# A selected-weight residual product on one core: the weights in eight transfers, the last stores in pairs

## The chip, the core and the metric

The kernel runs on one NeuronCore of a Trainium2 chip. The core has a TensorE (PE) for matrix products, a VectorE (DVE), a ScalarE (ACT), a GpSimd (POOL) and a SyncE (SP), each with its own instruction stream. Data moves between HBM and the on-chip memory SBUF (128 partitions) by 16 DMA engines, which all queues share. Here SyncE issues the small loads and all stores, ScalarE issues all loads of `x`. The metric is the device time of one execution in microseconds.

## What is computed

```python
def reference(x, itok_B_0_7, L0_cond_weights):
    # x (128, 128, 1024) f32, itok_B_0_7 (128,) int32 in 0..7, weights (8, 128, 128) f32
    w = L0_cond_weights[itok_B_0_7]
    return x + jnp.einsum('bct,bcd->bdt', x, w)
```

For each of 128 batch entries a 128 x 1024 matrix `x[b]` is multiplied by one of eight 128 x 128 weight matrices, chosen by the entry's index, and the product is added to `x[b]`. The input and the output are 67.1 MB each.

## The kernel before

A tile is H x G = 2 x 2 matrices of `x`, 2 MB, 16 KB in each of the 128 partitions. There are NT = 32 tiles and SLOTS = 12 slots in SBUF (`x_all`), which the tiles take in turn. The sum is written in place: a slot is loaded, the products are added into it, and it is stored from there.

All waits between engines are written out by hand with semaphores:

- **Loads** (L200 to L204, on ScalarE's queue). Each matrix is a transfer of 512 KB of its own, `load`, taken from HBM in 32 runs of 16 KB. From tile 12 on, the loads of tile i wait until the slot's last store, that of tile i - 12, has landed. So the stores of tiles 0 to 19 are waited for by loads, those of tiles 20 to 31 are not.
- **Ready** (L206 to L211, GpSimd): waits for a tile's loads and tells TensorE.
- **Weights** (L181): all eight matrices, 512 KB, are loaded once at the start into `w_all`, by one transfer on SyncE, in rows of 512 B. VectorE waits for it at L222, then copies the chosen matrices into `ws` (`place`, L153).
- **Products** (`multiply`, L162): for each half tile (two matrices) four products into PSUM. **Adds** (`add`, L174): VectorE adds a half tile of 128 x 2048 from PSUM into the slot and counts it in `s_added`; then it places the next weights.
- **Stores** (L213 to L218, on SyncE's queue). Tile i's store (2 MB) waits in `s_added` for tile i + BEHIND, four tiles further, as long as i is under NT - BEHIND - 2 = 26. Tiles 26 to 30 wait for themselves alone, but are behind tile 25's store in the queue. The last tile is stored in three parts: 1 MB (two matrices) after its first half's add, 0.5 MB after its second, and the last matrix, 0.5 MB, by L238.
- **End** (L235 to L245): ScalarE waits for each of the last twelve slots' stores, and the program's end waits for the last one.

Engines issue in their own program order, so what is behind a wait on SyncE waits too. `transfer` (L52) is the helper through which loads and stores are issued; their recorded line is L59, that of the helper.

Of the kernel before, what the change touches and what calls it, by code (L numbers as in the profile page):

```python
# [30 lines left out]
G = 2  # L31
H = 2
# [5 lines left out]
P_SLOTS = 2  # L38

BEHIND = 4  # L40

DMA = 16

IDLE = 3

ROWS = 4

ALIGN = 4096
QUEUES = {mybir.EngineType.SP: "qSPDynamicHW", mybir.EngineType.Activation: "qActDynamicHW"}
# [2 lines left out]
def transfer(nc, engine, out, in_):  # L52

    later, nc._always_lower_symbolic_ap = nc._always_lower_symbolic_ap, False
    ins, outs = engine.lower_ap_dma(in_), engine.lower_ap_dma(out)
    nc._always_lower_symbolic_ap = later
    return engine.add_instruction(  # L59
        mybir.InstDMACopy(  # L60
            name=nc.get_next_instruction_name(),
            engine=engine.engine,
            ins=ins,
            outs=outs,
            mode="Copy",
            cce_op=ALU.bypass,
            queue=QUEUES[engine.engine],
        )
    )


@with_exitstack
def kernel(
    ctx: ExitStack,
    tc: tile.TileContext,
    x: bass.AP,
    subjects: bass.AP,
    weights: bass.AP,
    out: bass.AP,
):  # L80
    nc = tc.nc
    B, C, T = x.shape
    S, _, D = weights.shape
    NT = B // (G * H)

    def sbuf(name, *shape, dtype=F32):
        return ctx.enter_context(nc.sbuf_tensor(name, list(shape), dtype)).ap()


    room = -(nc.sbuf_base + -nc.sbuf_base % 32) % ALIGN  # L90
    if room:
        sbuf("room", C, room // 4)
    x_all = sbuf("x_all", C, SLOTS * H * G * T)
    xs = [
        x_all[:, i * H * G * T : (i + 1) * H * G * T].rearrange("c (q t) -> c q t", t=T)
        for i in range(SLOTS)
    ]
    w_all = sbuf("w_all", C, S, D)
    ws = [sbuf(f"w{i}", C, 1, D) for i in range(H * G)]
    zeros = sbuf("zeros", C, N)  # L100
    given, near, wrap = (sbuf(name, 1, B, dtype=I32) for name in ("given", "near", "wrap"))
    index = sbuf("index", 1, B + H * G, dtype=I32)
    ps = [
        ctx.enter_context(nc.psum_tensor(f"ps{i}", [D, G, T], F32)).ap() for i in range(P_SLOTS)
    ]

    s_given = tc.alloc_semaphore("s_given")
    s_wall = tc.alloc_semaphore("s_wall")
    s_index = tc.alloc_semaphore("s_index")
    s_zeros = tc.alloc_semaphore("s_zeros")  # L110
    s_product = tc.alloc_semaphore("s_product")
    s_added = tc.alloc_semaphore("s_added")

    s_ready = tc.alloc_semaphore("s_ready")
    s_go = tc.alloc_semaphore("s_go")

    s_slot = [tc.alloc_semaphore(f"s_slot{k}") for k in range(SLOTS)]
    s_head = tc.alloc_semaphore("s_head")

    def emptied(i):  # L120
        turns = i // SLOTS
        return DMA * (H * G + 1) * turns - (DMA * G if i >= SLOTS and i % SLOTS == 0 else 0)

    def load(engine, i, q):
        transfer(
            nc,
            engine,
            xs[i % SLOTS][:, q, :],
            x[i * H * G + q].rearrange("(a r) t -> a (r t)", r=ROWS),
        ).then_inc(s_head if i * H * G + q < G else s_slot[i % SLOTS], DMA)  # L130

    def store(i, q0, q1):
        b = i * H * G
        transfer(
            nc,
            nc.sync,
            out[b + q0 : b + q1].rearrange("g d t -> d g t"),
            xs[i % SLOTS][:, q0:q1, :].rearrange("d (o g) t -> d o (g t)", g=q1 - q0),
        ).then_inc(s_slot[i % SLOTS], DMA)

    def subjects_of(i):
        _, subject = nc.values_load_multi_w_load_instructions(
            index[0:1, i] if isinstance(i, slice) else index[0:1, bass.ds(i * (H * G), H * G)],
            engines=[mybir.EngineType.DVE],
            min_val=0,
            max_val=S - 1,
            skip_runtime_bounds_check_because="the index is clamped on the chip above",
        )
        return subject

    def place(h, subject):
        for q in range(h * G, (h + 1) * G):
            copy = nc.vector.tensor_copy(ws[q], w_all[:, bass.ds(subject[q], 1), :])  # L153
        copy.then_inc(s_go, 1)

    def multiply(slot, h):
        nc.tensor.wait_ge(s_go, 1).then_inc(s_go, -1)
        nc.tensor.wait_ge(s_ready, 1).then_inc(s_ready, -1)  # L158
        for q in range(h * G, (h + 1) * G):
            for t in range(0, T, N):  # L160
                at = slot * (H * G * T) + (q * T + t)
                mm = nc.tensor.matmul(  # L162
                    ps[h][:, q % G, t : t + N],
                    ws[q][:, 0, :],
                    x_all[:, bass.ds(at, N)],
                    start=True,
                    stop=True,
                )
        mm.then_inc(s_product, 1)

    def add(slot, h):
        mine = x_all[:, bass.ds(slot * (H * G * T) + h * G * T, G * T)]
        nc.vector.wait_ge(s_product, 1).then_inc(s_product, -1)  # L173
        nc.vector.tensor_tensor(  # L174
            mine, ps[h].rearrange("d g t -> d (g t)"), mine, ALU.add
        ).then_inc(s_added, 1)

    with tc.tile_critical():  # L178

        nc.sync.dma_start(given, subjects.rearrange("(o b) -> o b", o=1)).then_inc(s_given, DMA)  # L180
        nc.sync.dma_start(w_all, weights.rearrange("s c d -> c s d")).then_inc(s_wall, DMA)  # L181

        nc.vector.memset(zeros, 0.0).then_inc(s_zeros, 1)  # L183
        nc.tensor.wait_ge(s_zeros, 1)
        for _ in range(IDLE):
            nc.tensor.matmul(  # L186
                ps[P_SLOTS - 1][:, G - 1, :N], zeros[:, :D], zeros, start=True, stop=True
            )

        nc.vector.memset(index[:, B:], 0).then_inc(s_index, 1)  # L193
        nc.vector.wait_ge(s_given, DMA)
        nc.vector.tensor_scalar(near, given, -S, S - 1, ALU.max, ALU.min).then_inc(s_index, 1)  # L195
        nc.vector.wait_ge(s_index, 2)
        nc.vector.tensor_scalar(wrap, near, 0, S, ALU.is_lt, ALU.mult).then_inc(s_index, 1)  # L197
        nc.vector.wait_ge(s_index, 3)
        nc.vector.tensor_tensor(index[:, :B], near, wrap, ALU.add).then_inc(s_index, 1)  # L199
        for i in range(NT):  # L200
            if i >= SLOTS:
                nc.scalar.wait_ge(s_slot[i % SLOTS], emptied(i))
            for q in range(H * G):
                load(nc.scalar, i, q)  # L204

        for i in range(NT):  # L206
            if i == 0:
                nc.gpsimd.wait_ge(s_head, DMA * G).then_inc(s_ready, 1)
                nc.gpsimd.wait_ge(s_slot[0], DMA * G).then_inc(s_ready, 1)
            else:  # L210
                nc.gpsimd.wait_ge(s_slot[i % SLOTS], emptied(i) + DMA * H * G).then_inc(s_ready, H)  # L211

        for i in range(NT):  # L213
            behind = BEHIND if i < NT - BEHIND - 2 else 0
            for h in range(H):
                if i == NT - 1 or h == H - 1:
                    nc.sync.wait_ge(s_added, (i + behind) * H + h + 1)
                    store(i, h * G if i == NT - 1 else 0, (h + 1) * G - (i * H + h == NT * H - 1))  # L218


        nc.vector.wait_ge(s_index, 4)
        nc.vector.wait_ge(s_wall, DMA)  # L222
        subject = subjects_of(slice(0, H * G))
        for h in range(H):
            place(h, subject)
        with nc.vector.Fori(0, NT) as turn:  # L226
            subject = subjects_of(turn + 1)
            for h in range(H):
                add(turn % SLOTS, h)
                place(h, subject)  # L230
        with nc.tensor.Fori(0, NT) as turn:
            for h in range(H):
                multiply(turn % SLOTS, h)

    with tc.tile_critical() as waits:  # L235
        for i in range(NT - SLOTS, NT):
            nc.scalar.wait_ge(s_slot[i % SLOTS], emptied(i + SLOTS) + (DMA if i == NT - 1 else 0))
    last = nc.sync.dma_start(out[B - 1], xs[(NT - 1) % SLOTS][:, H * G - 1, :])  # L238

    tc.add_manual_dep(  # L240
        last.ins,
        waits.name,
        mybir.DependencyInfo(mybir.DependencyClass.NoSync, mybir.DependencyReason.SCHED_ONLY),
        reason="the end of the program waits for it",
    )  # L245
# [27 lines left out]
```

## Time and profile before

| what | value |
|---|---|
| time, median of 3 runs (lowest to highest) | 323.61 us (323.46 to 323.78) |
| the profiled execution: time | 323.36 us |
| the profiled execution: span from first to last instruction | 321.6 us |
| mean granted TensorE clock | 0.909 |
| PE busy | 250.4 us (78%) |
| DVE busy | 165.7 us (52%) |
| moved by DMA | 134.76 MB in 12083 packets, mean 419 GB/s |
| loads of `x` on ScalarE's queue | 128 of 512 KB, median 35.5 us from issue to landing |
| stores on SyncE's queue | 31 of 2 MB, 1 of 1 MB, 2 of 0.5 MB; those of 2 MB median 16.2 us to landing |
| load of the weights | 1 of 512 KB, 5.2 us to landing |

Busy times are shares of one span and overlap each other. A share of 16 engines is the time that a queue's packets took, summed over all DMA engines, as a share of 16 times the stretch. "To landing" runs from the issue of a transfer to the arrival of its last completion, the time spent behind other transfers included. DMA issues are not counted as busy time of the engine that issues them.

### The profile page before, as it was taken

Reading aid. Unit: us, or ns where it says so; the run is one execution under the profiler, and the core shown is the slowest. Engines: PE = TensorE matmul, PEld = TensorE weight load, DVE = VectorE, ACT = ScalarE, POOL = GpSimd, SP = SyncE. Lnnn points to the kernel's source line nnn. Section 1 sums busy time; section 2 is a strip of 40 time slices with the busy share of each in tenths; the row PEclk is TensorE's granted clock in tenths of the full one; section 3 lists DMA queues with packets and bytes.
Section 4 is the critical chain, followed back from the end, with each engine's and each line's share of the span. In section 5 each row is a group of like instructions: output and inputs, shape, how many; then the busy total and the mean of one; then the engine's idle time right before and its main releaser. Section 6 shows DMA issues by size and latency. Waiting matters only on the chain. (4 is left out here: it accounts for less than half of the span.)

```text
span 321.6 us, 2379 instructions
## 1 busy us (share of the span) xinstructions
PE 250.4 (78%) x518; PEld 102.7 (32%) x518; DVE 165.7 (52%) x202; POOL 0.2 (0%) x4
## 2 busy tenths in 40 slices
PE   6999999999979676864989748899957969649100
PEld 2444444444433232321434313344312424214000
DVE  2377667767773266156267544167735237562300
POOL 0000000000000000000000000000000000000000
PEclk9999999999998699799799998599989799997755
DMA  7999999999999999999999999999999999999997
GB/s 279 430 424 424 426 424 406 428 428 430 424 424 426 423 428 426 426 428 426 428 428 428 424 426 426 426 426 426 428 428 426 430 428 426 424 426 426 428 426 300
DMA packets 12083, 134.76 MB, mean 419 GB/s; under 512 B 2609, under 2 KB 3634, under 8 KB 3890
## 3 DMA queue, kind: packets, MB, share of 16 engines
q1 hardware_dynamic: 5938, 67.64, 49.7%
q10 hardware_dynamic: 6144, 67.12, 49.6%
q14 instruction: 1, 0.01, 0.0%
HBM read 67.63 MB, written 67.11 MB: 419 GB/s over the span
## 5 line engine op out<-in xcount | busy, mean ns | idle before, releaser
L162 PE MATMUL ps<-x_all,w 128*128 x512 | 244.9, 636 | 46.4 <-PEq L158 30.8
L174 DVE TENSOR_TENSOR x_all<-ps,x_all 128x2048 f32 x64 | 146.7, 2291 | 129.5 <-DVEq L173 129.5
L162 PEld LDWEIGHTS ps<-x_all,w 128*128 128x128 f32 x512 | 100.9, 202 | 191.2 <-issue 190.7
L153 DVE COPY w<-w_all 128x128 f32 x132 | 23.2, 218 | 4.4 <-DMA w_all<-in_L_cond_weights_dram 4.4
L186 PE MATMUL ps<-zeros 128*128 128x512 f32 x6 | 5.5, 1088 | 1.7 <-DVE zeros L183 1.7
L186 PEld LDWEIGHTS ps<-zeros 128*128 128x128 f32 x6 | 1.9, 330 | 3.7 <-issue 2.1
L183 DVE MEMSET zeros<- 128x512 f32 x1 | 0.5, 485 | 1.0 <-SPq L178 1.0
L195 DVE TENSOR_SCALAR near<-given 1x128 int32<-1x128 int32 x1 | 0.2, 214 | 0.6 <-DMA given<-in_itok_B_dram 0.6
L199 DVE CUSTOM_DVE_ANT_0 index<-near,wrap 1x256 uint16<-1x256 uint16 x1 | 0.3, 280 | 0.0
L197 DVE TENSOR_SCALAR wrap<-near 1x128 int32<-1x128 int32 x1 | 0.2, 216 | 0.0
L260 POOL MEMSET const-bfloat16-1.0<- 128x1 bf16 x1 | 0.1, 102 | 0.0
L260 POOL MEMSET const-uint8-127<- 128x1 uint8 x1 | 0.1, 102 | 0.0
L260 POOL MEMSET const-float32-0.0<- 128x1 f32 x1 | 0.1, 99 | 0.2 <-issue 0.2
L260 POOL MEMSET const-float32-1.0<- 128x1 f32 x1 | 0.1, 99 | 0.0
L260 DVE BASE_LOAD x1 | 0.0, 15 | 0.1
L193 DVE MEMSET index<- 1x4 int32 x1 | 0.1, 62 | 0.0
## 6 DMA issues: line engine op xcount, KB each, us to landing
x_all<-in_x_dram ACTq DMA_DIRECT2D x128, 512.0 KB, 35.5
out_dram<-x_all SPq DMA_DIRECT2D x31, 2048.0 KB, 16.2
out_dram<-x_all SPq DMA_DIRECT2D x1, 1024.0 KB, 20.5
out_dram<-x_all SPq DMA_DIRECT2D x2, 512.0 KB, 18.3
w_all<-in_L_cond_weights_dram SPq DMA_DIRECT2D x1, 512.0 KB, 5.2
given<-in_itok_B_dram SPq DMA_DIRECT2D x1, 0.5 KB
```

The source lines that it names most:

```text
L153: copy = nc.vector.tensor_copy(ws[q], w_all[:, bass.ds(subject[q], 1), :])
L162: mm = nc.tensor.matmul(ps[h][:, q % G, t : t + N], ws[q][:, 0, :], x_all[:, bass.ds(at, N)], start=True, stop=True,)
L174: nc.vector.tensor_tensor(mine, ps[h].rearrange("d g t -> d (g t)"), mine, ALU.add).then_inc(s_added, 1)
L183: nc.vector.memset(zeros, 0.0).then_inc(s_zeros, 1)
L186: nc.tensor.matmul(ps[P_SLOTS - 1][:, G - 1, :N], zeros[:, :D], zeros, start=True, stop=True)
L193: nc.vector.memset(index[:, B:], 0).then_inc(s_index, 1)
L195: nc.vector.tensor_scalar(near, given, -S, S - 1, ALU.max, ALU.min).then_inc(s_index, 1)
L197: nc.vector.tensor_scalar(wrap, near, 0, S, ALU.is_lt, ALU.mult).then_inc(s_index, 1)
L199: nc.vector.tensor_tensor(index[:, :B], near, wrap, ALU.add).then_inc(s_index, 1)
L260: nc = _bacc.Bacc("TRN2", target_bir_lowering=False, num_devices=1)
```

## The change

The weights are loaded by eight transfers of 64 KB, one for each matrix, on the same queue. Each is read from HBM in 16 runs of 4 KB (eight rows of 512 B each) and written to one row of 512 B in each of 128 partitions. VectorE waits for all eight.

`store` now covers n whole tiles. Tiles 0 to 19 are stored one by one and wait as before for four tiles further. Tiles 20 to 31 are stored in pairs of neighbouring slots, 4 MB each. Pairs 20 and 22 wait for the fourth tile behind the pair's own last one (tiles 25 and 27); pairs 24, 26, 28 and 30 wait for their own adds alone. The last pair, tiles 30 and 31, is the program's last transfer, so the split of the last tile into three parts goes. ScalarE's waits at the end are five, one for each pair before the last.

```diff
@@ -38,12 +38,16 @@
 P_SLOTS = 2
 
 BEHIND = 4
+LAST = 8
+
+PAIR = 2
 
 DMA = 16
 
 IDLE = 3
 
 ROWS = 4
+W_ROWS = 8
 
 ALIGN = 4096
 QUEUES = {mybir.EngineType.SP: "qSPDynamicHW", mybir.EngineType.Activation: "qActDynamicHW"}
@@ -129,14 +133,14 @@
             x[i * H * G + q].rearrange("(a r) t -> a (r t)", r=ROWS),
         ).then_inc(s_head if i * H * G + q < G else s_slot[i % SLOTS], DMA)
 
-    def store(i, q0, q1):
-        b = i * H * G
-        transfer(
+    def store(i, n):
+        at = i % SLOTS * H * G * T
+        return transfer(
             nc,
             nc.sync,
-            out[b + q0 : b + q1].rearrange("g d t -> d g t"),
-            xs[i % SLOTS][:, q0:q1, :].rearrange("d (o g) t -> d o (g t)", g=q1 - q0),
-        ).then_inc(s_slot[i % SLOTS], DMA)
+            out[i * H * G : (i + n) * H * G].rearrange("g d t -> d g t"),
+            x_all[:, at : at + n * H * G * T].rearrange("d (o t) -> d o t", o=n),
+        )
 
     def subjects_of(i):
         _, subject = nc.values_load_multi_w_load_instructions(
@@ -178,7 +182,13 @@
     with tc.tile_critical():
 
         nc.sync.dma_start(given, subjects.rearrange("(o b) -> o b", o=1)).then_inc(s_given, DMA)
-        nc.sync.dma_start(w_all, weights.rearrange("s c d -> c s d")).then_inc(s_wall, DMA)
+        for k in range(S):
+            transfer(
+                nc,
+                nc.sync,
+                w_all[:, k, :],
+                weights[k].rearrange("(a r) d -> a (r d)", r=W_ROWS),
+            ).then_inc(s_wall, DMA)
 
         nc.vector.memset(zeros, 0.0).then_inc(s_zeros, 1)
         nc.tensor.wait_ge(s_zeros, 1)
@@ -210,16 +220,15 @@
             else:
                 nc.gpsimd.wait_ge(s_slot[i % SLOTS], emptied(i) + DMA * H * G).then_inc(s_ready, H)
 
-        for i in range(NT):
-            behind = BEHIND if i < NT - BEHIND - 2 else 0
-            for h in range(H):
-                if i == NT - 1 or h == H - 1:
-                    nc.sync.wait_ge(s_added, (i + behind) * H + h + 1)
-                    store(i, h * G if i == NT - 1 else 0, (h + 1) * G - (i * H + h == NT * H - 1))
+        for i in [*range(NT - SLOTS), *range(NT - SLOTS, NT, PAIR)]:
+            n = 1 if i < NT - SLOTS else PAIR
+            nc.sync.wait_ge(s_added, (i + n + (BEHIND if i < NT - LAST else 0)) * H)
+            if i + n < NT:
+                store(i, n).then_inc(s_slot[i % SLOTS], DMA)
 
 
         nc.vector.wait_ge(s_index, 4)
-        nc.vector.wait_ge(s_wall, DMA)
+        nc.vector.wait_ge(s_wall, DMA * S)
         subject = subjects_of(slice(0, H * G))
         for h in range(H):
             place(h, subject)
@@ -233,9 +242,9 @@
                 multiply(turn % SLOTS, h)
 
     with tc.tile_critical() as waits:
-        for i in range(NT - SLOTS, NT):
-            nc.scalar.wait_ge(s_slot[i % SLOTS], emptied(i + SLOTS) + (DMA if i == NT - 1 else 0))
-    last = nc.sync.dma_start(out[B - 1], xs[(NT - 1) % SLOTS][:, H * G - 1, :])
+        for i in range(NT - SLOTS, NT - PAIR, PAIR):
+            nc.scalar.wait_ge(s_slot[i % SLOTS], emptied(i + SLOTS))
+    last = store(NT - PAIR, PAIR)
 
     tc.add_manual_dep(
         last.ins,
```

## The prediction

> **What bounds the kernel now.** I read the page's slices and its DMA part first, then SyncE's own waits, then the time line at the end, then stretches of the span and the packets of single stretches.
>
> The slices: the first row is the busy share of the 16 DMA engines in tenths, the second what they moved.
>
> ```profile
> DMA  7999999999999999999999999999999999999997
> GB/s 279 430 424 424 426 424 406 428 428 430 424 424 426 423 428 426 426 428 426 428 428 428 424 426 426 426 426 426 428 428 426 430 428 426 424 426 426 428 426 300
> ```
>
> Only the first, the seventh and the last slice fall short. SyncE's waits (total us, times, longest) and the last rows of the time line:
>
> ```profile
> SPq L59 <- DVE x_all L174: 275.7, 30, 44.6
> SPq L269 <- DMA out_dram<-x_all: 17.9, 1, 17.9
> ```
> ```profile
> 298.74 2.29 DVE L174 TENSOR_TENSOR x_all<-ps,x_all 128x2048 f32 x1 [0.81 <-DVEq L173]
> 300.95 0.35 DVE L153 COPY w<-w_all 128x128 f32 x2
> 301.06 0.48 SPq L59 DMA_DIRECT2D out_dram<-x_all  x1
> 302.26 0.37 SPq L238 DMA_DIRECT2D out_dram<-x_all  x1
> ```
>
> The last add ends at 301.03, the span at 321.6. For these 20.5 us only DMA runs, and the program's end waits 17.9 us for the last store. The chain of waits on the page says nothing here, since it follows engines and not transfers. Stretches (length, busy of PE, PEld, DVE and POOL, clock, DMA share, GB/s):
>
> ```profile
> 0.00:8.00 8.00, 5.49 (x6) 1.85 (x6) 1.84 (x10) 0.20 (x4) 1.00 0.77 279
> 8.00:16.00 8.00, 7.56 (x17) 3.25 (x18) 2.92 (x4) 0.00 (x0) 1.00 1.01 428
> 16.00:314.00 298.00, 237.35 (x496) 97.62 (x494) 160.91 (x189) 0.00 (x0) 0.91 1.01 426
> ```
>
> From 8 to 314 us the DMA engines are full, whether they load alone (8 to 16 us: 428), load and store, or store alone (292 to 313 us: 428). So time is bytes over about 427 GB/s plus what is lost at both ends. A later or earlier wait in between is worth nothing unless it leaves both queues empty. **Start:** the first data moves at 2.2 us; by 8 us 2.23 MB have moved, worth 2.23/0.427 = 5.2 of those 5.8 us. So 0.6 us is lost there, and no change to the weights' load alone can win more. **End:** from 319.0 to 320.4 only 126 GB/s flow (0.18 MB, worth 0.4 of 1.4 us), the engines running out one by one; then 1.2 us of completion.
>
> **Part 1, the weights.** Now one transfer of 512 KB, 1024 packets of 512 B. The packets of 3.4 to 6.2 us (queue: packets, MB, share of 16 engines), and those of 292 to 313 and of 318 to 320.4 us:
>
> ```profile
> q1 hardware_dynamic: 1040, 0.52, 62.8%
> ```
> ```profile
> q1 hardware_dynamic: 612, 8.98, 100.6%
> ```
> ```profile
> q1 hardware_dynamic: 173, 0.60, 61.1%
> ```
>
> The first: 0.628 x 2.8 x 16 = 28.1 us over 1024 packets is 27.5 ns for 512 B. The second, 548 packets of 16 KB: 1.006 x 21 x 16 / 548 = 0.617 us. The third, 146 packets of 4 KB: 0.611 x 2.4 x 16 / 146 = 0.161 us. The small packets among the counts (16 per transfer) signal completion and are included. The weights cost 1024 x 27.5 ns / 16 = 1.76 us of all engines now. Afterwards they are 128 packets of 4 KB, each spread over eight rows of 512 B in SBUF, a form that the trace does not have. Low price: that of the 4 KB store packet, 128 x 161 / 16 = 1.29 us. High price: each row like a 512 B packet, 8 x 27.5 = 220 ns, 1.76 us. The nearest row speaks for the low end: a load of x has 16 KB runs over four rows of 4 KB and goes at 428 GB/s, just as stores do, so splitting at the destination was free there. I take 1.29: **a gain of 0.47 us**, bounds 0 and 0.47 (0.6 if the whole hole goes). It lies on the path, because the engines are full from there on.
>
> Seven more transfers add 7 x 16 completion packets, and the stores below lose 8 x 16: nil.
>
> Issue: SyncE issues the weights in 0.42 us at 1.36. Eight take 8 x 0.42 to 8 x 0.65 (the slowest store issue without a full queue), so the last is issued by 4.8 to 6.6 us. Behind them SyncE has nothing until the store at 46.4 us. Landing: now 5.2 us after issue, with the first copy of weights at 7.35. The first 512 KB load of x took 3.6 us from issue to landing, so the last weights land at some 7 to 10 us instead of 6.5, and VectorE, with PE behind it (first product at 8.26), starts 1 to 3 us later. The cover is large: the first 48 loads and the weights are 25.7 MB, which keep the engines full to 8 + (25.7 - 2.23)/0.426 = 63 us; the first data moves 1.3 us after an issue, so store 0 may be issued as late as 61.8. It is issued at 46.4. **15 us of cover**; 0 us on the path.
>
> **Part 2, the last stores.** Every slot reloaded (tiles 0 to 19) keeps its wait, hence all loads keep theirs. Tiles 20 to 31 are no longer waited for by any load. Pair 20 waits for tile 25's adds (store 20 waited for tile 24's), pair 22 for tile 27's; pairs 24 and 26 then pass at once; pair 28 waits for tile 29's, pair 30 for tile 31's. Behind each wait on SyncE there are only later stores. Can both queues run dry? While pair 20 or 22 waits, the loads go alone: the last of them was issued at 250.1 and landed 39.2 us later, so there is a deep backlog, and loads alone fill the engines. After the loads end (289.3 now) stores alone must. With both busy, 64 to 160 us, stores get 56.6% and loads 44.0%: 23.05 MB against 17.86 MB in 96 us, 240 and 186 GB/s.
>
> Reckoning on: store 19 lands at 222.3 + 14.6 = 236.9 and tile 25 is added by 236.7, so pair 20 runs from about 239 to 256.5; tile 27 is added by about 259 (261.0 now), since loads ran alone for some 2 us. Loads run alone again until about 261, then share with 12.6 MB of pairs 22 to 26. From 236.9 there were 21 loads left (11 MB); the two stretches alone take 3 of 7 MB at full rate, the shared ones do the rest by 286 to 289. Tile 31 is then added at 298 to 301. Pair 30 needs 4.19 MB / 0.427 = 9.8 us, an issue to first data of 1.3 and an end of 1.4 (320.2 to 321.6): 12.5 of the 20.5 us after the last add, **8 us of cover**. If the last add came d later than 8 us after its present time, the end would come d - 8 later.
>
> What remains is packets. The last two matrices' worth go in 4 KB and the two before in 8 KB packets: 1.02 MB of the latter between 314.1 and 316.6, at 97.0%, is 2.43 us for all engines. With 256 x 161 / 16 = 2.58 that is 5.0 us, against 128 x 617 / 16 = 4.94 in 16 KB packets. **A gain of 0.1 us**; the other bound is the unevenness at the very end, where a last packet of 617 instead of 161 ns may add 0.45 us or the pairs may even it out for the same gain.
>
> **Sum:** 0.47 + 0.1 = 0.57 off. The profiled execution took 323.36 (span 321.6 and 1.8 around it), so 322.8; it stood 0.25 under the median, so on that 323.04. With a part of the price of the destination rows unknown I round to **323.1**.
>
> The page "DMA: Bandwidth & Descriptors" of the Trainium skill (Rules for kernel authors) says to merge many small transfers into one large, and calls those under 64 KB mostly overhead; eight of 64 KB sit at that edge, and by it the weights would come later, which the last rival prices from rows.
>
> **Rivals.** A measurement of this kernel tells about 0.2% (0.65 us) from no change; that is the bound below.
> 1. *The destination rows decide.* Each 512 B row is written as its own piece, and the weights gain nothing. For it: no such packet in the trace; against: x's loads. Time 323.5.
> 2. *Both ends mend further.* The hole of 0.6 us in the start closes wholly, because x's second load no longer stands behind 64 small packets per engine, and the uneven end (1.0 us lost) shrinks by half. For it: both holes are there; against: the first packets are slow by themselves, and engines drift apart over the whole run. 0.6 + 0.1 + 0.4 = 1.1 off: 322.5.
> 3. *The last pair finds the queue empty.* Tile 30's store, issued at 287.7 now, waits for tile 31, and stores 22 to 27 queue at one time against the last loads. If the last nine loads (4.7 MB, 25 us at 186 GB/s) got under 4.7/(25 + 8) = 142 GB/s, engines would idle ahead of pair 30. At 120 GB/s they take 39 us, 6 beyond the cover: 329. Against it: the shares hold over 96 us.
> 4. *Small transfers are served one by one.* Eight times 3.6 us is 28.8 instead of 5.2 us; the first copy would be 23.6 us later, 8 beyond the cover, and the time 331. It decides from 15 us on. Against it: 24 loads were issued in 15.5 us and none waited for the one before. [...]
>
> **Chances.** Forecast 0.42 (322.96 to 323.5, within 0.2%); rival 1 0.10, also no change; rival 2 0.36, faster; rivals 3 and 4 0.08 and 0.04, slower. So faster 0.36, same 0.52, slower 0.12. The range runs from 322.3 (rival 2 and a little more) to 323.9 (rival 1 and the uneven end at its worst); rivals 3 and 4 stay outside. The forecast's own range is 322.8 to 323.5.
>
> **What would show it.** The first slice above 279 GB/s by 0.2 MB / 8 us, i.e. over 300; 128 packets of 4 KB with 161 ns or up to 220; the first copy of weights 1 to 3 us later with no thinner slice at 50 to 65 us; DMA at 9 in every slice between 240 and 314 us; the last add before 309. A slice below 420 late in the span would prove part 2 wrong, a first slice unchanged part 1.

## The result, and the profile after

| | before | after |
|---|---|---|
| median of 9 runs | 323.61 us | 324.75 us |
| ratio of the times, 95% interval | | 1.003 (1.0018 to 1.0042) |
| profiled execution: time, span | 323.36, 321.6 us | 325.17, 323.4 us |
| DMA packets, moved | 12083, 134.76 MB | 10915, 134.76 MB |

The change makes the kernel slower by 0.3%, about 1 us; no change was forecast, with a gain of 0.5 us. One run of the changed kernel stood apart at 328.71 us and is left out of the ratio. The profiled execution is one of the longer ones, 1.8 us over that of before. The slices of the changed kernel's page, DMA busy and GB/s:

```profile
DMA  6999999999999999999999999999999999999995
GB/s 238 392 422 426 430 424 432 426 424 426 428 428 430 428 423 422 430 428 426 430 426 422 430 428 428 430 424 424 428 426 426 434 426 424 424 430 426 432 428 253
```

The first slice has 238 GB/s where before had 279 and more was expected, and the second 392 where before had 430. From there on all is full up to the last. The dip of the seventh slice of before (406) is gone. Stretches of the span (length, busy times, clock, DMA share, GB/s):

```profile
0.00:8.00 8.00, 4.41 (x6) 1.70 (x6) 1.22 (x6) 0.20 (x4) 1.00 0.67 238
8.00:16.00 8.00, 0.00 (x0) 0.00 (x0) 0.45 (x4) 0.00 (x0) 0.52 1.02 391
8.00:20.00 12.00, 3.55 (x4) 1.50 (x5) 0.63 (x4) 0.00 (x0) 0.51 1.01 399
...
50.00:55.00 5.00, 5.00 (x13) 2.02 (x12) 3.07 (x6) 0.00 (x0) 1.00 0.99 419
55.00:65.00 10.00, 10.00 (x24) 4.22 (x23) 7.42 (x9) 0.00 (x0) 1.00 1.01 426
65.00:314.00 249.00, 195.44 (x409) 80.52 (x408) 133.10 (x156) 0.00 (x0) 0.90 1.01 427
```

The same stretches of before, as far as they differ (its first two stand in the prediction):

```profile
8.00:20.00 12.00, 11.56 (x27) 5.00 (x28) 5.54 (x7) 0.00 (x0) 1.00 0.99 422
...
50.00:55.00 5.00, 5.00 (x13) 2.09 (x12) 3.07 (x7) 0.00 (x0) 1.00 0.95 383
55.00:65.00 10.00, 10.00 (x25) 3.96 (x23) 7.56 (x9) 0.00 (x0) 1.00 1.02 433
```

In the first column of busy times of the changed kernel PE has nothing from 8 to 16 us: the products have not begun. Up to 20 us the changed kernel moves 238 x 8 + 399 x 12 = 6.69 MB, before 279 x 8 + 422 x 12 = 7.30 MB (the rates of the first 8 us and of 8 to 20 us). The 0.61 MB are worth 1.4 us at 427 GB/s: the loss arises at the start. From 50 to 65 us some of it comes back: 419 x 5 + 426 x 10 against 383 x 5 + 433 x 10 is 0.11 MB more, some 0.3 us. The first store is issued at 57.1 here and at 46.4 in before. At the end (the time line's last rows and SyncE's waits):

```profile
296.45 2.29 DVE L178 TENSOR_TENSOR x_all<-ps,x_all 128x2048 f32 x1 [0.81 <-DVEq L177]
298.66 0.35 DVE L157 COPY w<-w_all 128x128 f32 x2
299.31 0.60 SPq L63 DMA_DIRECT2D out_dram<-x_all  x1
```
```profile
SPq L278 <- DMA out_dram<-x_all: 22.4, 1, 22.4
```

The last add ends at 298.7, earlier than before, and the program's end waits 22.4 us for the last pair: no engine's work and no wait of a store for an add is what ends last there. The eight loads of the weights (durations of the issues, first and last start; then time to landing):

```profile
L63 SPq DMA_DIRECT2D w_all<-in_L_cond_weights_dram x8: 574/594/682, 1.3 to 5.9; - x8
DMA to landing us min/median/max: 3.6/7.3/8.8
```

The last is issued at 5.9 and lands at 14.7, not at 7 to 10, and VectorE's first copy follows there:

```profile
15.55 0.63 DVE L157 COPY w<-w_all 128x128 f32 x4 [12.58 <-DMA w_all<-in_L_cond_weights_dram]
```

### The profile page after: what moved, and what is told of

Its sections match the earlier page's. It is cut to its first block, busy times and chain, and to the rows that moved or that the text cites. A ratio compares the mean times of both kernels' runs of the same rounds, so it can differ in the third digit from the quotient of the medians.

```text
span 323.4 us, 2375 instructions
## 1 busy us (share of the span) xinstructions
PE 248.4 (77%) x518; PEld 102.5 (32%) x518; DVE 165.7 (51%) x202; POOL 0.2 (0%) x4
## 2 busy tenths in 40 slices
DMA packets 10915, 134.76 MB, mean 417 GB/s; under 512 B 2593, under 2 KB 2594, under 8 KB 2722
## 5 line engine op out<-in xcount | busy, mean ns | idle before, releaser
L196 PE MATMUL ps<-zeros 128*128 128x512 f32 x6 | 4.4, 893 | 1.7 <-DVE zeros L193 1.7
```

The lines of the kernel that those rows point to most:

```text
L196: nc.tensor.matmul(ps[P_SLOTS - 1][:, G - 1, :N], zeros[:, :D], zeros, start=True, stop=True)
```

## The experiments

Each ratio is to runs of before on the same chip, taken in turn with those of the kernel. "Moved by 20 us" is the rate of the first 8 us times 8 plus that of 8 to 20 us times 12.

| kernel | time, median | ratio (95%) | GB/s 0 to 8, 8 to 20 us | moved by 20 us | store 0 issued |
|---|---|---|---|---|---|
| before | 323.4 | | 279, 422 | 7.30 MB | 46.4 |
| weights only | 324.77 | 1.0038 (1.0025 to 1.0051) | 232, 405 | 6.72 MB | 56.0 |
| pairs only | 323.34 | 0.9998 (0.9989 to 1.0007) | 275, 429 | 7.35 MB | 46.5 |
| eight, rows of 512 B | 340.18 | 1.0507 (1.0484 to 1.0529) | 226, 427 | 6.93 MB | 72.6 |
| computing late | 323.36 | 0.9993 (0.9984 to 1.0002) | 277, 426 | 7.33 MB | 56.6 |
| weights on ScalarE's queue | 325.07 | 1.0078 (1.0044 to 1.0112) | 221, 389 | 6.44 MB | 59.7 |
| weights spaced | 330.02 | 1.0208 (1.0177 to 1.024) | 236, 403 | 6.72 MB | 65.5 |
| rows of 1 KB | 327.87 | 1.0143 (1.0119 to 1.0167) | 245, 416 | 6.95 MB | 63.0 |
| pairs, computing late | 323.15 | 0.9987 (0.9977 to 0.9996) | 279, 423 | 7.31 MB | 57.9 |
| all eight behind x | 326.41 | 1.0092 (1.0076 to 1.0109) | 246, 393 | 6.68 MB | 62.3 |
| the one transfer behind x | 347.1 | 1.0733 (1.0715 to 1.0751) | 246, 418 | 6.98 MB | 81.0 |

**Which part.** Each part of the change alone.

```diff
-        nc.sync.dma_start(w_all, weights.rearrange("s c d -> c s d")).then_inc(s_wall, DMA)
+        for k in range(S):
+            transfer(
+                nc,
+                nc.sync,
+                w_all[:, k, :],
+                weights[k].rearrange("(a r) d -> a (r d)", r=W_ROWS),
+            ).then_inc(s_wall, DMA)
...
-        nc.vector.wait_ge(s_wall, DMA)
+        nc.vector.wait_ge(s_wall, DMA * S)
```

> Only the weights' load is changed (eight transfers of 64 KB in 16 runs of 4 KB), the stores are those of before. Theory A, the loss comes from the start: 324.5 to 325 us, ratio to before about 1.003; 0 to 8 us at about 240 GB/s, 8 to 16 us at about 390; the last weights land some 13 us after the first issue, and the last data moves about 1 us later than in before. Theory B, the loss comes from the pairs at the end: 323.1 to 323.6, with no loss of rate in the first 16 us that is not made good.

Measured: 324.77, the whole loss. The second kernel is the changed one with these lines as before:

> Only the stores are changed (pairs, waits), the weights come in one transfer as before. Theory A: 323.3 to 323.7, ratio 0.999 to 1.000, first slice 279 GB/s as before, the last engine finishes about as late after the others as in before (1 us). Theory B: 324.5 or more, with the last engine some 2 us behind the first as in the changed kernel.

Measured: 323.34, no difference that can be told. Its end, stretches as above:

```profile
314.00:319.00 5.00, 0.00 (x0) 0.00 (x0) 0.00 (x0) 0.00 (x0) 0.50 0.99 419
319.00:320.40 1.40, 0.00 (x0) 0.00 (x0) 0.00 (x0) 0.00 (x0) 0.50 0.09 35
```

It runs at 419 GB/s up to 319.0 (before 404) and has less left then, 35 GB/s against 126, so it is done no later than before. The last store waits in its queue even longer than in the changed kernel:

```profile
294.47 0.60 SPq L63 DMA_DIRECT2D out_dram<-x_all  x1
...
SPq L272 <- DMA out_dram<-x_all: 25.0, 1, 25.0
```

Theory A stands, B falls: the pairs cost nothing, and the weights all of it.

**Is it the late start of computing?** Before, with one wait more for VectorE:

```diff
         nc.vector.wait_ge(s_wall, DMA)
+        nc.vector.wait_ge(s_slot[1], DMA * H * G)
```

> Before, but VectorE waits, before its first copy of weights, also for the four loads of the second tile, so that all computing starts some 8 us later, as in the changed kernel, and the start of the DMA is untouched. Theory C, the late first product costs: 324.5 or more, with a stretch between 45 and 70 us under 400 GB/s. Theories A and B (15 us of cover): 323.4 to 323.8, within 0.1% of before, store 0 issued at about 55.

Measured: 323.36. The first copy is at 16.1 instead of 7.35 us, store 0 is issued at 56.6 instead of 46.4, and it costs nothing. The same wait on the kernel with pairs:

> The pairs of the changed kernel, the weights in one transfer as before, and VectorE's first copy held until the second tile has landed. If the thinner stretch at 50 to 55 us (383 GB/s in before) comes from the first stores starting while ScalarE's queue is still filling, it goes and 0.3 us with it: 323.0 to 323.2. If it is any first store's, it only moves to 60 to 70 us: 323.3 to 323.5.

Measured: 323.15, ratio 0.9987. It beats both kernels by a hair, with an interval that ends at 0.9996. The rate from 50 to 65 us no longer dips, but part of the dip is found again later (414 GB/s in the tenth slice, 72 to 80 us, after store 0 at 57.9). The kernel of before with the same late start has an interval that includes no change, so it is not shown that later first stores alone give the 0.3 us.

**The number of transfers or their form?** Eight transfers with rows of 512 B on both sides:

```diff
-        nc.sync.dma_start(w_all, weights.rearrange("s c d -> c s d")).then_inc(s_wall, DMA)
+        for k in range(S):
+            transfer(nc, nc.sync, w_all[:, k, :], weights[k]).then_inc(s_wall, DMA)
```

> Before, with the weights in eight transfers of 64 KB that keep rows of 512 B on both sides, so 128 packets of 512 B each. Theory A1, the number of transfers is at fault (each queues for its turn beside the loads of x): slow as the changed kernel, 324.5 or more, last weights landing at 12 us or later, 8 to 16 us under 420 GB/s. Theory A2, the form is at fault (a packet of 4 KB that is written to eight rows): 323.4 to 323.8, with the full rate from 8 us on.

Neither theory as a whole: 340.18, with the delay of A1 and the rate of A2. The slices and the weights' landings of this kernel:

```profile
DMA  7999999527999999999999999999999999999994
GB/s 239 422 421 428 425 429 431 248 124 266 433 423 421 433 427 424 417 431 429 423 417 431 431 423 419 435 429 429 415 433 429 423 421 433 431 421 417 423 429 178
```
```profile
L59 SPq DMA_DIRECT2D w_all<-in_L_cond_weights_dram x8: 577/602/891, 1.4 to 6.3; - x8
DMA to landing us min/median/max: 3.5/13.9/24.7
```

The last weights land at 31.0, store 0 is issued at 72.6, and in the eighth to tenth slice both queues run dry: the cover that the prediction worked out is used up. Here the weights wait beside the loads of `x`, while the rate from 8 to 20 us (427) does not suffer. With runs of 1 KB (`W_ROWS = 2`):

> Eight transfers of 64 KB in runs of 1 KB (two rows each): 4 data packets and 1 completion for each engine and transfer. Theory T, queues take turns packet by packet, completions counted: each transfer waits 5 turns of x (0.41 us a turn, from 2 packets of 0.617 and a completion per load), so they land some 2.2 us apart (1.1 in the changed kernel, 3.9 with rows of 512 B) and the last at 19 to 21 us; with 14 us of delay the 15 us of cover just hold: 323.9 to 325.5. Rival: landing is set by issue and latency, then the last lands by 15 us as in the changed kernel.

Measured: 327.87; the last weights land at 6.1 + 15.4 = 21.5, near the 19 to 21 expected (the spacing is in the table under "Turns"). The time is above the range given: store 0, issued at 63.0, is just past the cover, and the price there rises faster than reckoned.

**Two queues?** The eight transfers of 4 KB runs, one behind each of the first eight loads on ScalarE's own queue, in place of the one transfer on SyncE's:

```diff
...
                 load(nc.scalar, i, q)
+                k = i * H * G + q
+                if k < S:
+                    transfer(
+                        nc,
+                        nc.scalar,
+                        w_all[:, k, :],
+                        weights[k].rearrange("(a r) d -> a (r d)", r=W_ROWS),
+                    ).then_inc(s_wall, DMA)
...
```

> Before, with the eight 64 KB transfers (16 runs of 4 KB) on ScalarE's queue, one behind each of the first eight loads of x, so that weights and x are in one queue in order and SyncE issues nothing there. Theory Q, the loss comes from two queues at the start (descriptors for both at once, and the taking of turns): 323.2 to 323.6 us, 0 to 8 us at 275 GB/s or more, 8 to 14 us as in before (410 by this count). Theory F, the loss comes from the form (4 KB written to eight rows holds an engine up): still 377 to 390 GB/s from 8 to 14 us, 324.2 or more.

Measured: 325.07, 377 GB/s from 8 to 14 us. Theory Q falls, the form costs in one queue too. Its twelve runs form two groups, nine of 324.6 to 325.5 and three of 329.1 to 329.3; the ratio takes in both and so lies above that of the medians. What parts them is not known. Spaced out on SyncE's queue (two at once, two after 2, two after 4 and two after 8 loads of `x`):

```diff
+        after = {2: (s_head, G), 4: (s_slot[0], G), 6: (s_slot[1], H * G)}
         for k in range(S):
+            if k in after:
+                nc.sync.wait_ge(after[k][0], DMA * after[k][1])
             transfer(
...
```

> The weights as in the changed kernel, but SyncE issues two at once, two when the first 2 loads of x have landed, two after 4 and two after 8, the last four therefore some 10 to 15 us into the span. Theory G, the hole of the first 8 us comes from issuing eight transfers beside the loads of x: 0 to 8 us at 265 GB/s or more instead of 232 to 238. Theory F: each pair still costs rate when its packets pass, together 0.5 to 0.7 us, so 323.9 to 324.4. If neither, 324.7 as with the eight in a row. The last weights land at 17 to 18 us, 11 us late, inside the cover.

Measured: 330.02. Theory G fails: with packets of only two of the eight in the first 8 us (the next two are issued at 7.5 and 8.0) these still have 236 GB/s. And the last weights land 6.7 us behind their issue, at 23.9 instead of the 17 to 18 expected, so this kernel too runs past the cover.

**Whose hole is it?** All eight, and in another kernel the one transfer of before, issued only when the first two loads of `x` have landed:

```diff
+        nc.sync.wait_ge(s_head, DMA * G)
```

> The eight transfers of the changed kernel, issued only when the first two loads of x have landed (stores as before the change). Theory G, the hole of the first 8 us comes from transfers of weights prepared between the first loads of x: then 0 to 8 us moves about 2.37 MB, 295 GB/s, x alone. Rival: the hole is the start of x itself, covered in before by the packets of the one transfer: then 0 to 8 us stays at or under 250. Theory F: the form costs again when it passes, 8 to 30 us moves 0.3 MB or more less than in before. The last weights land at 20 to 24 us, over the cover: 327 to 330.

> Before, with the one transfer of the weights issued when the first two loads of x have landed. Theory T, turns: 64 data packets and a completion for each engine, each waiting a turn of x of 0.41 us: 27 to 29 us, so it lands at 36 to 38 and the first copy follows there; far over the cover, 343 to 348. Rival, a large transfer is served in one go: it lands at 12 to 14 us, 323.3 to 323.8. For its rate from 10 to 35 us: 425 or more, as packets of 512 B were cheap in the run with rows of 512 B.

Measured: 326.41, a little less than expected, and 347.1, where the weights land at 39.2 instead of 36 to 38 us. First the kernel with all eight (stretches, then packets from 10 to 20 us, in which all weights pass: the 256 packets of q1 are 128 of weights and as many completions):

```profile
0.00:8.00 8.00, 5.42 (x6) 1.85 (x6) 1.21 (x6) 0.20 (x4) 1.00 0.74 246
10.00:20.00 10.00, 0.00 (x0) 0.00 (x0) 0.00 (x0) 0.00 (x0) 0.51 1.02 393
```
```profile
q10 hardware_dynamic: 311, 3.41, 87.0%
q1 hardware_dynamic: 256, 0.52, 14.8%
```

Then the one transfer behind `x`, stretches and landing:

```profile
0.00:8.00 8.00, 5.49 (x6) 1.85 (x6) 1.21 (x6) 0.20 (x4) 1.00 0.75 246
```

```profile
L182 SPq DMA_DIRECT2D w_all<-in_L_cond_weights_dram x1: 417/417/417, 6.2 to 6.2; - x1
DMA to landing us min/median/max: 33.0/33.0/33.0
```

The rival of theory G is right. With no weights on the way (both kernels have none of their packets in the first 8 us), the loads of `x` alone move 246 x 8 = 1.97 MB by 8 us. Full rate from 2.2 us on would be 5.8 x 0.427 = 2.48 MB, so their own start has a hole of some 1.2 us. In the trace of the one transfer behind `x`, the first 16 packets of `x` are slow, as in before, and nine more that start from 5.1 to 5.5 us take 1.3 to 2.0 us instead of 0.61. Before has none of these late ones, and it moves more: 279 x 8 = 2.23 MB, 0.52 of them weights, so `x` had moved 1.71 MB. **The one transfer cost `x` only 1.97 - 1.71 = 0.26 MB, 0.6 us.** The eight cost it from 10 to 20 us 4.27 - 3.41 = 0.86 MB (4.27 is 10 us at 427 GB/s), **2.0 us**, or 2.0 x 16 / 128 = 0.25 us for each packet. The difference, 1.4 us, is what the start loses.

Where do the 2.0 us lie? Packets of `x` in before (8 to 40 us) and beside rows of 512 B (the kernel of eight transfers with such rows, 8 to 30 us):

```profile
q10 hardware_dynamic: 1250, 13.65, 100.7%
```
```profile
q10 hardware_dynamic: 814, 8.91, 95.4%
```

A packet of `x` has 16 KB, so these are 833 packets of 1.007 x 32 x 16 / 833 = 0.62 us, and 544 of 0.954 x 22 x 16 / 544 = 0.62 us. Beside the eight transfers of 4 KB runs there are 208, of 0.870 x 10 x 16 / 208 = 0.67 us. The weights' own packets take 0.148 x 10 = 1.48 us of all engines, 0.185 us each with their completions. The other part is that 208 packets of `x` last 0.05 us longer: 208 x 0.05 / 16 = 0.65 us. Together this is 2.1 us, which agrees with what `x` lost. Packets of 512 B do not lengthen those of `x`, nor do those of 1 KB over two rows (0.62 us from 9 to 20 us in that kernel). Why those of 4 KB over eight rows do is not known.

**The form alone.** ScalarE's first load waits until all eight have landed (`x` starts some 7 us later):

```diff
+        nc.scalar.wait_ge(s_wall, DMA * S)
         for i in range(NT):
             if i >= SLOTS:
```

> The eight transfers in 16 runs of 4 KB with nothing beside them: ScalarE's first load waits for all weights. If the form is slow by itself, its 128 packets take about 0.25 to 0.3 us each in the trace; if it is slow only beside loads of x, 0.16 to 0.18. Whole time about 6 to 8 us over before (x starts that much later).

Measured in a single run: 330.17, and the packets from 2.0 to 8.2 us:

```profile
q1 hardware_dynamic: 256, 0.52, 32.1%
```

0.321 x 6.2 x 16 / 128 = 0.25 us for each packet of 4 KB, with nothing beside it. That does not show that the form is slow by itself. The engines pause between these packets (they are busy for 32% of the time), single ones take from 0.156 to 0.39 us in the trace, and the first 16 packets of `x` after the pause take 0.82 to 1.34 us instead of 0.61. The mean may be that of any packets after a pause.

**Turns.** A turn of `x` is (2 x 0.617 + 0.01) / 3 = 0.41 us, since each load gives an engine two packets and a completion. If the engine changes queue at each packet, completions counted, a transfer with n packets of weights on each engine takes n + 1 turns and its own packets:

| weights' transfer | turns | reckoned | measured spacing or landing |
|---|---|---|---|
| 16 runs of 4 KB (all eight behind x) | 2 | 0.83 + 0.25 = 1.1 us | (19.7 - 12.0) / 7 = 1.1 us |
| 64 runs of 1 KB | 5 | 2.1 + 0.2 = 2.3 us | (21.5 - 4.8) / 7 = 2.4 us |
| 128 rows of 512 B | 9 | 3.7 + 0.2 = 3.9 us | (31.0 - 4.9) / 7 = 3.7 us |
| one transfer, 1024 rows, behind x | 65 | 26.9 + 1.8 = 28.7 us | 33.0 us from issue to landing |

Ends are issue plus landing time of the first and the last transfer; 0.2 and 1.8 are packets of 27.5 ns. The last row includes some 4 us until the first turn. The same count gives the stores' share: 8 packets to 6 of `x` for 9 turns each, 4 to 3, against 240 to 186 GB/s in before. The page "DMA: Bandwidth & Descriptors" of the Trainium skill (Queues, rings and completion order) has the engines go round between queues packet by packet, a packet being some 9 to 17 descriptors; in these runs the spacings fit a turn of one packet as the profile counts them (one run of 16 KB, 4 KB or less), not a group of such a size, and the measurement decides.

## Why the prediction was wrong

**Right: what bounds the kernel.** Rate times bytes and the two ends; computing 9 to 10 us later is free (323.36), and every slice but those of the start and the end is full.

**Right: part 2.** Neither queue ran dry, and the last add, forecast at 298 to 301, ended at 298.7. The 0.1 us that fewer small packets were to save cannot be told from nothing (0.9998).

**Wrong: the price of the weights' new packets**, "that of the 4 KB store packet, 128 x 161 / 16 = 1.29 us", with 220 ns as the dearest. By what `x` lost it is 2.0 us in all, 0.25 us each, outside both bounds. The packets' own time is not the error: 1.48 us, 185 ns each, lies between the bounds. What failed is that the sum counted this time alone. The packets of `x` beside them took 0.67 instead of 0.62 us, 0.65 us for all engines, and the prediction has no term for that. The row chosen as nearest, loads of `x` over four rows of 4 KB, said nothing of rows of 512 B. Rival 1, that the destination rows decide, came nearer and put it at no gain; its price, that of eight separate packets of 512 B, was too low as well.

**Wrong: the price of what was removed**, 1.76 us on the path "because the engines are full from there on". The transfer cost `x` 0.6 us: without it the start of `x` has a hole of its own, twice the 0.6 us that the prediction saw. So the sum of part 1 reads not -1.76 + 1.29 = -0.47 but -0.6 + 2.0 = +1.4 us. This second error is the larger: with it alone the sum would be -0.6 + 1.29 = +0.7 us, with the first alone -1.76 + 2.0 = +0.2 us. With the 0.3 us that come back from 50 to 65 us, 1.1 are left, which is what the medians show. Rival 2 saw the hole of before, but had it close with the change; it grew.

**Mis-sized: when the weights land.** "VectorE ... starts 1 to 3 us later"; its first copy is 8.2 us later (15.55 against 7.35), by the turns, which the prediction did not know. It cost nothing, as the cover was there, and its 15 us were about right: with store 0 at 59.7 us the median has no loss beyond the start (1.7 us over before, against 0.86 MB or 2.0 us less by 20 us; three of the twelve runs have some 4 us more), at 62.3 there are 1.6 us more than that (3.0 less 1.4). What was too low is the price past 61.8: store 0 at 65.5, 72.6 and 81.0 cost some 5, 16 and 23 us besides the start, up to 5 us more than the delay beyond the cover. Rival 4 was right in kind only: transfers are not served one by one, but where turns make them late enough (rows of 512 B) the loss was 16.8 us, more than the 8 that the rival priced.

**Not settled.** In the profiled execution the last data moves some 1.8 us later than in before, 0.7 more than start and stores explain: a few engines finish after the others. Of the runs with a loss at the start some show this and some do not, and no run was made for it. What makes the slow packets in the start of `x`, and why before does not have the late ones, was not tried either.

## What to carry to other kernels

Before pricing a transfer that is to be replaced, find out what else could have moved while it ran: the packets of the one transfer cost a third of their time (0.6 of 1.76 us), because the loads alone would not have filled the engines. Price new packets by what the stream beside them loses, not by their own time. A longer run on one side bought nothing here, where the other side stayed cut into rows of 512 B. A small load beside a stream of large packets waited here for a turn of these (0.41 us) at each of its own packets, so count its packets per engine, or issue it before the stream has a backlog.

## What the runs showed of the hardware beyond that

A packet of 4 KB from HBM over eight rows of 512 B cost the loads beside it 0.25 us, 0.185 of them in its own record; the same bytes as eight packets of 512 B took 8 x 27.5 = 220 ns, and a store's packet of 4 KB from one row 161 ns. One and the same transfer of 512 KB landed after 5.2 us when it met a nearly empty queue and after 33.0 us when it met a full one beside it. The Trainium skill's page "DMA: Bandwidth & Descriptors" (Specifications) gives 512 B as the least size for full rate; here packets of 512 B ran at 512 / 27.5 = 18.6 B/ns for each engine against 16384 / 617 = 26.6.
